# A four-layer graph network on one core: the planner that writes out the order of its instructions gets other costs, rules and ranks

## The chip, the core and the metric

The kernel runs on one core of a Trainium2 chip. The metric is the device time of one execution in microseconds (us), the median of several runs. TensorE (PE) multiplies, VectorE (DVE), ScalarE (ACT) and GpSimd (POOL) do the elementwise work, and the queue of SyncE (SP) issues nearly all transfers.

## What is computed

There are 128 batches. Each is a matrix x of 128 nodes by 512 features in float32; `adj` is one 128 x 128 matrix of edge weights for all of them. Four layers follow one another, each of the form `x = layernorm(x + layer(x))` over the features, with no dependence between batches:

```
layer 0:  A = adj @ x ; C = adj @ x + b ; out[:, n] = max over m of relu(A[:, m] + (C - A)[:, n])
layer 1:  q, k, v = x@Wq+bq, x@Wk+bk, x@Wv+bv ; 8 heads of 64
          softmax(q k^T / 8 + (1-adj) * -1e9) v, then @ Wo + bo
layer 2:  h = x@W ; e = leaky_relu(s1 + s2^T) * adj ; elu(softmax(e) @ h + beta*h)
layer 3:  (D^-1/2 adj D^-1/2) @ (x @ weight) + bias
```

With one adj for both weights of layer 0, its output is a row maximum of `adj @ x` plus b, cut off at zero.

## The kernel before, in words

**Batches in pairs.** Batches b and b+1 form a pair. The six products with 512 x 512 weights (Q, K, V, Y for Wo, U for layer 2's W, Z for layer 3's weight) are made once per pair with Strassen's scheme: `seven` (L619 ff.) writes seven half-size products P1 to P7 into three PSUM tiles px, py, pz. px holds P1 and then P2, py P6, P7, P4, and pz P5, P3. ScalarE copies P1 out (`u`, `uL`), VectorE makes U2, U3, C21, C22 and C12. GpSimd makes four sums S1 to S4 of the operand (L651). Three differences of weight quarters are made once per weight (`T`, L631 to L635): on VectorE for Q and K, on GpSimd for the others.

**Steps of one batch.** LD loads x (L411). A multiplies by adj (L764), R takes the row maximum (L770), ST0 the statistics (L581), Q0, P0 and AP0 normalise (L590 to L609; the power is on GpSimd, L604). MX1 writes x to a DRAM buffer dx (L788). RL reads it back as x2 for the residual (L802). For attention x must be turned to features by nodes: MX2 reads dx back in four transfers with 32-row blocks (L794) and TX turns the blocks on VectorE (L830). For the first pair only (`early`, b < 2) PX, PT and PTE do this without DRAM: a VectorE copy (L810), four TensorE transposes (L819), another copy (L824). SC makes the scores (L855), M, SM1, EXP, SMR, SMN the softmax (L871 to L900), MS1, MS2 and TS turn the probabilities through DRAM (L904, L912, L920), O multiplies them by v (L930). Then come Y, layer norm, the layer 2 attention (L, E, EZ, E1, EE, E2, BT, BE, GT), U, its elu (U1, UE, U2, UP), layer norm, NX (L1075), Z, layer norm and OUT (L1106). SC and O use half of TensorE's array (64 rows or columns), all other products use the whole.

**One-time steps.** Weights, biases and broadcast rows are fetched one after another on SP in the order of `FETCH`; Wq and its biases are fetched on ScalarE's queue ahead of everything else. ROW multiplies bv by Wo (L524). LOG makes ten VectorE instructions for layer 2's score vectors (L538, L543), LOG1 turns them on TensorE (L556). MASK, BQ and NORM prepare mask, scaled bias and normalised adj.

**The order.** Every engine works its queue strictly in order of issue, and the kernel writes that order itself. `STEPS` gives each step an engine, a cost in us, the steps it comes after, and the buffers it takes with the readers that free them (`POOLS` has their numbers; `+` is both batches of a pair, `-1` the batch before, `@` batches 0 and 1). `list_order` then plays the whole kernel: again and again it takes, of all steps whose inputs are listed, the one that can start first. On TensorE ties go to the lowest `rank`, which is the batch number plus the step's entry in `LAG`, less an entry in `LEAD` for the last pairs; on other engines to the step that was ready first, less its `soon`:

```
if s.engine == "PE":
    key = (t, rank(*k) - (CLOSE if mode and s.mode else 0.0), k)
else:
    key = (t, ready[k] - s.soon, k)
```

A transfer is an SP step of 0.4 us, whose reader is given a fixed delay (`("LD", 3.1)`). A switch between whole and half array costs 0.1. The planner decides only the order; on the chip, semaphores make each instruction wait for its inputs, and an instruction that waits holds up all behind it on its engine.

Of the kernel before, what the change touches and what calls it, by code (L numbers as in the profile page):

```python
# [10 lines left out]
ALU = mybir.AluOpType  # L11
# [3 lines left out]
S = 32  # L15
# [10 lines left out]
CLOSE = 0.5  # L26


class Step:
# [9 lines left out]
    def __init__(self, engine, cost, *after, takes=(), soon=0.0, batches=None, port=False, mode=""):  # L39
        self.port = port or engine == "POOL"  # L40
        self.mode = mode
        self.engine, self.cost, self.after = engine, cost, after
        self.takes, self.soon = dict(takes), soon
        self.batches = batches or (lambda b: True)
# [17 lines left out]
def list_order(steps, rank, pools, n):  # L62
# [5 lines left out]
    for s, b in todo:  # L68
        for a in steps[s].after:
            a, late = a if isinstance(a, tuple) else (a, 0.0)  # L70
            for k in steps[s].others(a, b):
                if k in todo:
                    missing[s, b].add(k)
                    users.setdefault(k, []).append(((s, b), late))
    can = {k for k in todo if not missing[k]}
    free, ends, taken, order, mode = {}, {}, {p: [] for p in pools}, [], ""
    while todo:
        best = None
        for k in can:
            s = steps[k[0]]  # L80
            t = max(ready[k], free.get(s.engine, 0.0), free.get("port", 0.0) if s.port else 0.0)
            for p in s.buffers(k[1]):
                if len(taken[p]) >= pools[p]:
                    for r in taken[p][-pools[p]]:
                        t = max(t, ends.get(r, 1e9) + SIGNAL)
            if t >= 1e9:
                continue
            if s.engine == "PE":
                key = (t, rank(*k) - (CLOSE if mode and s.mode else 0.0), k)
            else:  # L90
                key = (t, ready[k] - s.soon, k)
            if best is None or key < best:
                best = key
        t, _, k = best
        s = steps[k[0]]
        order.append((t, *k))
        ends[k] = t + s.cost
        if s.engine == "PE" and s.mode != mode:
            ends[k] += SWITCH
            mode = s.mode  # L100
        free[s.engine] = ends[k]
        if s.port:
            free["port"] = ends[k]
        todo.discard(k)
        can.discard(k)
        for p, readers in s.buffers(k[1]).items():
            ends_of = [r for a in readers for r in s.others(a, k[1])]
            taken[p].append([r for r in ends_of if r in missing])
        for u, late in users.get(k, ()):
            same = steps[u[0]].engine == s.engine and not late  # L110
            ready[u] = max(ready[u], ends[k] + late + (0.0 if same else SIGNAL))
            missing[u].discard(k)
            if not missing[u]:
                can.add(u)
# [11 lines left out]
def early(b):  # L126
    return b < 2


def late(b):  # L130
    return b >= 2
# [13 lines left out]
    "ROW": Step("PE", 3.5, "BV", ("BO", 4.0), takes={"tr": ("ROW1",)}, batches=first),  # L145
    "ROW1": Step("DVE", 0.7, "ROW", batches=first),
    "LOG": Step("DVE", 5.7, "BETA", ("A1", 4.0), batches=first, port=True),
# [7 lines left out]
    "LD": Step("SP", 0.4, "LD-1", ("LD-2", 8.0), takes={"x": ("MX1", "PX")}),  # L155
    "ST0": Step("DVE", 0.82, ("LD", 3.1), takes={"t0": ("AP0+",)}),
    "ADJ": Step("PE", 0.2, ("LD", 2.3), takes={"tr": ("ADJ1",)}, batches=first),
    "ADJ1": Step("DVE", 0.3, "ADJ", batches=first),
    "A": Step("PE", 0.87, ("LD", 3.1), "A-1", "ADJ1@", takes={"tr": ("R",)}),
    "R": Step("DVE", 0.82, "A", takes={"r": ("AP0+",)}),  # L160
    "Q0": Step("ACT", 1.2, "ST0+", "R+", soon=10, batches=even),
    "P0": Step("POOL", 0.58, "Q0", soon=10, batches=even),
    "AP0": Step("ACT", 1.03, "P0+", soon=20),
    "MX1": Step("SP", 0.4, "AP0", "MX1-1", takes={"dx": ("MX2+", "RL")}),

    "PX": Step("DVE", 0.6, "AP0", takes={"xB": ("PT",)}, soon=20, batches=early, port=True),
    "PT": Step("PE", 0.5, "PX", takes={"tr": ("PTE",)}, batches=early),
    "PTE": Step("DVE", 0.65, "PT", "PTE-1", soon=20, batches=early),
    "MX2": Step("SP", 2.6, ("MX1", 2.1), takes={"xB": ("TX",)}, batches=late),
    "RL": Step("SP", 0.4, ("MX1+", 2.1), takes={"x2": ("UP+",)}, batches=even),  # L170
    "C1": Step("POOL", 1.27, ("RL+", 3.0), "ROW1@"),
    "TX": Step("DVE", 0.65, ("MX2", 2.9), "TX-1", batches=late),
    "SC": Step("PE", 1.09, mode="row", takes={"sc": ("M",)}),
    "M": Step("DVE", 1.33, "SC", "MASK@", takes={"s": ("MS2",)}),
# [4 lines left out]
    "MS1": Step("SP", 0.4, "SMN", takes={"dp": ("MS2",)}),  # L179
    "MS2": Step("SP", 1.8, ("MS1", 2.7), takes={"sB": ("TS",)}),  # L180
    "TS": Step("DVE", 1.18, ("MS2", 3.8), takes={"sT": ("O",)}),
# [30 lines left out]
    "OUT": Step("SP", 0.4, "AP3"),  # L212
# [5 lines left out]
for i, name in enumerate(FETCH):  # L218
    STEPS[name] = Step("SP", 0.4, (FETCH[i - 1], 1.3) if i else ("LD@", 4.0), batches=first)
# [4 lines left out]
def sum_steps(n, engine_needs, readers):  # L224

    for i in range(4):
        needs = engine_needs if i == 0 else [f"{n}S{i}"]
        takes = {"SX" if n == "X" else "S": readers} if i == 0 else {}
        cost = 0.75
        STEPS[f"{n}S{i+1}"] = Step("POOL", cost, *needs, takes=takes, batches=even)  # L230


def seven_steps(n, sums, needs, weights, pool, out, add=(), turned=False, copy=False, T="POOL"):
# [10 lines left out]
    STEPS[n + "T"] = Step(T, 5.2 if T == "POOL" else 3.0, *weights, batches=first)  # L244
# [12 lines left out]
    step("P6", "PE", c, "S2", "P1", (n + "T@",), takes={"py": (n + "C21",)})  # L257
# [3 lines left out]
    step("P4", "PE", c, "U3")  # L261
# [25 lines left out]
for n, needs, letters in (  # L287
# [4 lines left out]
    "Q": seven_steps("Q", "X", ["TX+", "PTE+", "BQ@"], [("ADJ1", 9.0), "PTE+"], "xT", {"qT": ("SC+",)},  # L292
                     turned=True, T="DVE"),
    "K": seven_steps("K", "X", ["TX+", "PTE+", "BQ@"], [("WK3", 4.0)], "xT", {"kT": ("SC+",)},
                     turned=True, T="DVE"),
    "V": seven_steps("V", "X", ["TX+", "PTE+"], [("WV3", 4.0)], "xT", {"v": ("O+",)}, copy=True),
    "Y": seven_steps("Y", "Y", ["OE+"], ["ROW", ("WO3", 4.0)], "oT", {}, add=["C1+"]),
    "U": seven_steps("U", "U", ["GE+"], ["LOG", ("W23", 4.0)], "gT", {"x3": ("OUT+",)}, copy=True),
    "Z": seven_steps("Z", "Z", ["NE+"], [("W33", 4.0)], "nx", {}, add=["C3+"]),
}  # L300
STEPS["SC"].after = (*done["Q"], *done["K"])
# [7 lines left out]
    "A": 0.506, "QP4": 9.260, "KP1": 9.601, "QP1": 10.141, "QP6": 10.308, "QP2": 10.612,  # L309
    "QP7": 11.336, "QP5": 11.387, "QP3": 11.470, "KP6": 11.592, "KP2": 11.639,  # L310
    "KP7": 11.706, "KP4": 11.707, "KP3": 11.885, "KP5": 11.949, "VP6": 12.245, "SC": 12.416,
    "VP1": 13.139, "VP2": 13.218, "VP3": 13.390, "VP7": 13.434, "VP5": 13.540,
    "VP4": 13.603, "O": 15.187, "YP2": 16.207, "YP1": 16.635, "UP4": 16.678, "YP7": 16.681,
    "YP4": 16.877, "YP6": 17.006, "YP3": 17.007, "YP5": 17.021, "E": 17.459, "BT": 18.003,
    "GT": 18.470, "UP7": 18.991, "UP1": 19.286, "UP6": 19.912, "UP5": 20.037, "UP2": 20.403,
    "UP3": 20.409, "NX": 20.899, "ZP1": 22.103, "ZP6": 22.106, "ZP2": 22.151, "ZP3": 22.157,
    "ZP4": 22.409, "ZP7": 22.472, "ZP5": 22.856,
# [3 lines left out]
    "Q56": 0.53, "U56": 0.07, "A57": -0.03, "BT57": -0.1, "GT57": -0.06, "NX57": 2.33,  # L321
    "O57": -0.08, "Y57": 0.14, "BT58": -0.35, "E58": 0.31, "GT58": 0.72, "K58": 0.05,
    "NX58": -0.04, "O58": 0.4, "SC58": -1.4, "U58": 0.34, "V58": 1.06, "Y58": 2.36, "BT59": -0.24,
    "E59": -0.03, "K59": 0.5, "NX59": 1.93, "O59": 0.25, "Q59": -1.29, "SC59": 0.01, "U59": -0.55,
    "Y59": -0.04, "Z59": 0.01, "BT60": 0.03, "E60": 0.36, "GT60": 0.39, "K60": 0.03,
    "NX60": -0.22, "Q60": -0.03, "SC60": -0.01, "V60": 0.51, "A61": -3.65, "BT61": 0.32,
    "E61": 3.22, "GT61": -0.07, "K61": 2.69, "SC61": -0.11, "U61": -11.19, "V61": -0.03,
    "Y61": -0.11, "Z61": 0.22, "A62": -0.09, "BT62": -0.26, "E62": -0.69, "GT62": -1.7,
    "K62": 0.01, "NX62": 4.35, "O62": 0.18, "Q62": 0.09, "U62": -0.09, "V62": -3.72, "Y62": 0.36,
    "Z62": -0.17, "BT63": 5.89, "E63": 1.65, "K63": 0.46, "NX63": -0.37, "O63": 2.5, "Q63": -0.04,  # L330
    "SC63": 6.66, "U63": 0.09, "V63": -2.36, "Y63": -0.12, "Z63": -0.21,
# [11 lines left out]
def kernel(  # L343
# [117 lines left out]
    for part in (bq_part, bk_part, *wq_parts):  # L461
        fetch(nc.scalar, part)
# [156 lines left out]
    def seven(n, w, operand, sums, tag, result, added=None, bias=None, scale=1.0):  # L619
# [10 lines left out]
        def T(b):  # L630
            op = (nc.vector if n in "QK" else nc.gpsimd).tensor_tensor  # L631
            op(T3, W[1, 1], W[0, 1], ALU.subtract)
            op(T1, W[0, 1], W[0, 0], ALU.subtract)
            op(T2, W[1, 1], T1, ALU.subtract)
            op(T4, W[1, 0], T2, ALU.subtract)  # L635
# [114 lines left out]
        do[n + "T"], do[n + "u"], do[n + "uL"] = T, u, uL  # L750
# [368 lines left out]
    for i in range(2):  # L1119
        do[f"LOG1{'ab'[i]}"] = lambda b, i=i: LOG1(i)  # L1120
        do[f"LOG2{'ab'[i]}"] = lambda b, i=i: LOG2(i)
    with tc.manual_schedule():
# [46 lines left out]
```

## Time and profile before

| | |
|---|---|
| median of 3 runs | 3119.07 us (3118.03 to 3120.9) |
| the profiled execution | 3121.7 us, span of its instructions 3119.8 us |
| TensorE busy | 3059.5 us, 98% of the span, 21018 matmuls |
| VectorE, ScalarE, GpSimd busy | 2303.2 (74%), 2205.9 (71%), 1676.2 (54%) us |
| transfers | 312.91 MB, mean 100 GB/s |
| chain of work that ended last | PE 91%, DMA 3%, DVE 2%, ACT 2%, issue 1% |

"Busy" for TensorE is from the first to the last of pipelined matmuls, so a busy engine is not one at its peak. The granted clock (PEclk) is the share of full clock that TensorE got, 1.00 or 0.50 in any moment, and a mean in a stretch. In a line of the timeline the columns are start, duration, engine, source line, operation, what is written and read, shapes and the number of instructions merged. A bracket gives the idle time of the engine before it and what ended it. A line with SPq is SP's queue issuing a transfer. Names are those of the tiles: ps_a belongs to step A, px_Q to products P1 and P2 of Q, py_K to P6, P7, P4 of K, and so on; ps_x to PT, ps_wa to LOG1, ps_nx to NX. xB is MX2's target, x<-dx is RL.

### The profile page before, as it was taken

What the parts mean: (1) busy time and instruction counts of PE and PEld (TensorE: products, weight loads), DVE (VectorE), ACT (ScalarE), POOL (GpSimd) and SP (SyncE); (2) the same over time, 40 slices, a digit from 0 to 9 for tenths busy, and PEclk for the clock granted to TensorE, in tenths of its full rate; (3) what the DMA queues carried; (4) which work ended last, traced back from release to release, by engine and by line L of the source; (5) the groups of instructions that cost most, each with busy time, mean ns of one, the idle gap of its engine ahead of it and who ended that gap; (6) DMA issues with size and microseconds to landing.
All of it is one profiled execution on the core that took longest, in us unless ns stands there. A gap on an engine that the chain in (4) does not pass through costs nothing.

```text
span 3119.8 us, 61689 instructions
## 1 busy us (share of the span) xinstructions
PE 3059.5 (98%) x21018; PEld 2694.8 (86%) x21018; DVE 2303.2 (74%) x5416; ACT 2205.9 (71%) x7234; POOL 1676.2 (54%) x1946
## 2 busy tenths in 40 slices
PE   7999999999999999999999999999999999999996
PEld 4888888888888888888888888888888888898985
DVE  6777777777777777777777777777777777777774
ACT  3667777777777777777777777777777776776764
POOL 4344545555555555555555555555455555565565
PEclk8999999999999999999999999999999999999998
DMA  7432323323323323323333233233233232322220
GB/s 212 133 110 84 113 89 111 105 89 109 105 93 109 102 96 102 106 97 102 99 105 98 99 105 100 93 111 102 90 111 105 89 109 88 102 82 89 68 68 27
DMA packets 235611, 312.91 MB, mean 100 GB/s; under 512 B 27809, under 2 KB 157985, under 8 KB 235297
## 3 DMA queue, kind: packets, MB, share of 16 engines
q1 hardware_dynamic: 233520, 307.93, 30.3%
q8 instruction: 166, 2.72, 0.4%
q10 hardware_dynamic: 1776, 1.05, 0.2%
q14 instruction: 149, 1.21, 0.1%
HBM read 174.66 MB, written 134.22 MB: 99 GB/s over the span
## 4 chain that ended last, share of the span: by engine, by line
PE 91%; DMA 3%; DVE 2%; ACT 2%; issue 1%; POOL 0%; SPq 0%; POOLq 0%; DVEq 0%; ACTq 0%
PE py_Y L675 5%; PE py_U L675 5%; PE py_V L675 5%; PE py_Q L675 5%; PE py_Z L675 5%; PE py_K L675 5%; PE ps_s L855 4%; PE ps_o L930 4%; PE px_U L675 4%; PE ps_nx L1075 4%; PE pz_Q L675 4%; PE px_V L675 4%; PE px_Y L675 4%; PE ps_gT L1028 4%; PE pz_Y L675 3%; PE pz_Z L675 3%
## 5 line engine op out<-in xcount | busy, mean ns | idle before, releaser
L609 ACT ACTIVATE x<-x,off,rstd 128x512 f32<-128x512 f32 x512 | 416.7, 814 | 17.1
L886 ACT ACTIVATE s<-s,mx 128x128 f32<-128x128 f32 x1024 | 395.6, 391 | 27.3 <-DVE mx L880 27.3
L604 POOL TENSOR_TENSOR rstd<-rstd,neg_half 128x2 f32<-128x2 f32 x256 | 178.8, 699 | 388.9 <-ACT rstd L590 388.7
L581 DVE BATCH_NORM_STATS2 st<-x 128x6 f32<-128x512 f32 x512 | 349.1, 682 | 41.8 <-DMA x<-in_x 36.7
L900 ACT ACTIVATE s<-s,sm 128x128 f32<-128x128 f32 x1024 | 313.1, 391 | 19.7 <-DVE sm L895 19.6
L1089 POOL TENSOR_TENSOR x<-x,b_bc 128x512 f32<-128x512 f32 x128 | 163.2, 1276 | 255.4 <-PE ps_nx L1075 254.2
L1056 POOL TENSOR_TENSOR x<-x,x 128x512 f32<-128x512 f32 x128 | 163.6, 1278 | 176.6 <-DVE x L1052 169.9
L651 POOL TENSOR_TENSOR S_U<-gT 128x256 f32<-128x256 f32 x128 | 107.1, 836 | 228.0 <-ACT gT L940 228.0
L608 ACT ACTIVATE off<-off,rstd 128x1 f32<-128x1 f32 x512 | 145.5, 284 | 77.6 <-POOL rstd L604 77.5
L964 DVE SCALAR_TENSOR_TENSOR junk<-x,wa_bc 128x512 bf16<-128x512 f32 x256 | 184.2, 719 | 16.1 <-ACT x L609 10.6
L886 ACT ACTIVATION_READ_ACCUMULATOR s<-s,mx 128x1 f32 x1024 | 195.4, 191 | 0.0
L920 DVE STREAM_TRANSPOSE sT<-sB 128x1024 f32<-128x1024 f32 x128 | 159.2, 1244 | 34.9 <-PE ps_o L930 33.4
L651 POOL TENSOR_TENSOR S_Y<-oT 128x256 f32<-128x256 f32 x128 | 93.9, 733 | 139.8 <-PE pz_U L675 125.6
L806 POOL TENSOR_TENSOR x<-x,bo_bc 128x512 f32<-128x512 f32 x128 | 160.8, 1277 | 15.0 <-DMA x<-dx 14.8
L871 DVE TENSOR_TENSOR s<-ps_s,mask 128x512 f32<-128x512 f32 x256 | 163.4, 679 | 2.4 <-PE ps_s L855 2.1
L734 DVE TENSOR_TENSOR x<-py_U,u_U 128x256 f32<-128x256 f32 x192 | 81.1, 422 | 103.8 <-PE py_U L675 53.7
L880 DVE TENSOR_REDUCE mx<-s 128x8 f32<-128x1024 f32 x128 | 154.6, 1208 | 0.2
L675 PEld LDWEIGHTS px_Q<-xT,wq_sb 128*128 128x128 f32 x1024 | 129.3, 192 | 26.4 <-issue 23.7
L675 PEld LDWEIGHTS py_K<-SX_V,KT 128*128 128x128 f32 x1024 | 129.8, 193 | 24.5 <-issue 23.4
L855 PE MATMUL ps_s<-kT,qT 64*128 64x128 f32 x2048 | 148.9, 285 | 0.0
L1075 PE MATMUL ps_nx<-naT,x 128*128 128x128 f32 x1024 | 138.4, 280 | 10.5 <-ACT x L609 10.5
L855 PEld LDWEIGHTS ps_s<-kT,qT 64*128 64x128 f32 x2048 | 124.3, 187 | 26.1 <-issue 21.8
(186 smaller groups left out, 9116.0 us busy)
## 6 DMA issues: line engine op xcount, KB each, us to landing
dp<-s SPq DMA_DIRECT2D x128, 512.0 KB, 2.8
sB<-dp SPq DMA_DIRECT2D x512, 128.0 KB, 2.8
x<-in_x SPq DMA_DIRECT2D x128, 256.0 KB, 2.9
dx<-x SPq DMA_DIRECT2D x128, 256.0 KB, 2.1
x<-dx SPq DMA_DIRECT2D x64, 512.0 KB, 3.3
out_x<-x SPq DMA_DIRECT2D x128, 256.0 KB, 2.0
xB<-dx SPq DMA_DIRECT2D x504, 64.0 KB, 2.0
wk_sb<-in_L_gnn_Wk SPq DMA_DIRECT2D x4, 256.0 KB, 7.7
```

What stands on the lines that cost most here:

```text
L581: nc.vector.bn_stats(st, t)
L604: nc.gpsimd.tensor_tensor(r, r, neg_half.to_broadcast([P, 2]), ALU.pow)
L609: nc.scalar.activation(dst, src, AF.Identity, bias=shift, scale=scale)
L651: nc.gpsimd.tensor_tensor(s[:, i], x, y, op)
L675: nc.tensor.matmul(to, lhsT=one, rhs=two, start=(new and k == 0), stop=(k == 1), skip_group_check=True,)
L855: nc.tensor.matmul(scores[b][par][:, c, :], lhsT=qT[b][rows, c, cols], rhs=kT[b][rows, c, cols], start=True, stop=True,)
L871: nc.vector.tensor_tensor(by_head(s)[:, par * C : (par + 1) * C], ps.rearrange("p h (q s) -> p h q s", s=S), mask.rearrange("p (q s) -> p ...
L886: nc.scalar.activation(s[:, :, h], s[:, :, h], AF.Exp, bias=mx[:, h : h + 1], accum_out=sums[b][:, h : h + 1],)
L900: nc.scalar.activation(s[:, :, h], s[:, :, h], AF.Identity, scale=sm[:, h : h + 1])
L964: nc.vector.scalar_tensor_tensor(junk, x2[b][:, b % 2], 1.0, wa_bc[i], op0=ALU.mult, op1=ALU.mult, accum_out=s12[b][:, i : i + 1],)
L1056: nc.gpsimd.tensor_tensor(t, t, x2.pop(b)[:, b % 2], ALU.add)
L1075: nc.tensor.matmul(ps[:, c, :], lhsT=x3[b][:, b % 2, c * P : (c + 1) * P], rhs=naT, start=True, stop=True,)
```

## The change

The diff touches the planner, its tables, and the places that a step can be cut:

- **Costs of TensorE.** If TensorE was idle for more than REST = 1.4 us, steps that start within WAKE = 3.7 us cost double. A switch is counted only between whole and half array, not between SC and O. CLOSE, the bonus for a half-array step while the array is in halves, goes from 0.5 to 2.0 batches.
- **Transfers.** A step with `dma=(latency, time on the bus)` ends when a bus shared by all transfers has carried it. A reader without a delay of its own waits for that end.
- **rush.** On engines other than TensorE, steps of the first four batches' layer 0 and turning (40) and the operand sums of batches 0 and 2 (30) win ties. SP's MX1 has it too.
- **Turning.** `early` and `late` go from b < 2 to b < 4: batches 2 and 3 also take PX, PT, PTE instead of MX2, TX.
- **Weight sums.** T becomes four steps T0 to T3 of one instruction each (0.75 on VectorE, 1.34 on GpSimd). P6 needs T2, P4 needs T3.
- **Fetches.** The first eight pieces (Wk, Wv) follow each other by at least 1.0 us and start 2.0 us after the loads of batches 0 and 1 (1.3 and 4.0 before); the later ones follow by 3.0. Wq's four pieces become steps WQ0 to WQ3 on ScalarE.
- **Other.** SC also comes after the SC of the batch before; `s` is free after MS1, not MS2.
- **Ranks.** LAG and LEAD are new. A is 0.325 and the attention products lie 15.7 to 19.2 batches behind (9.3 to 13.6 before); the last Z product is at 28.3 (22.9). LEAD has 26 entries (62).

```diff
-CLOSE = 0.5
+CLOSE = 2.0
+REST, WAKE = 1.4, 3.7
...
-            a, late = a if isinstance(a, tuple) else (a, 0.0)
+            a, late = a if isinstance(a, tuple) else (a, None)
...
-                key = (t, ready[k] - s.soon, k)
+                key = (t, ready[k] - s.soon - (s.rush if k[1] < 4 else 0.0), k)
...
-        ends[k] = t + s.cost
-        if s.engine == "PE" and s.mode != mode:
-            ends[k] += SWITCH
+        cost = s.cost
+        if s.engine == "PE":
+            if t - free.get("PE", -9.0) > REST:
+                warm = t + WAKE
+            if t < warm:
+                cost *= 2
+            if bool(s.mode) != bool(mode):
+                cost += SWITCH
             mode = s.mode
-        free[s.engine] = ends[k]
+        ends[k] = free[s.engine] = issued = t + cost
+        if s.dma:
+            ends[k] = free["bus"] = max(t + s.dma[0], free.get("bus", 0.0)) + s.dma[1]
...
-            same = steps[u[0]].engine == s.engine and not late
-            ready[u] = max(ready[u], ends[k] + late + (0.0 if same else SIGNAL))
+            if steps[u[0]].engine == s.engine and not late and (late == 0.0 or not s.dma):
+                t = issued
+            elif late is None:
+                t = ends[k] + SIGNAL
+            else:
+                t = issued + late + SIGNAL
+            ready[u] = max(ready[u], t)
...
 def early(b):
-    return b < 2
+    return b < 4
...
-    "LD": Step("SP", 0.4, "LD-1", ("LD-2", 8.0), takes={"x": ("MX1", "PX")}),
-    "ST0": Step("DVE", 0.82, ("LD", 3.1), takes={"t0": ("AP0+",)}),
+    "LD": Step("SP", 0.4, ("LD-1", 0.0), ("LD-2", 8.0), takes={"x": ("MX1", "PX")}, dma=(2.55, 0.9)),
+    "ST0": Step("DVE", 0.82, "LD", takes={"t0": ("AP0+",)}, rush=40),
...
-    "A": Step("PE", 0.87, ("LD", 3.1), "A-1", "ADJ1@", takes={"tr": ("R",)}),
-    "R": Step("DVE", 0.82, "A", takes={"r": ("AP0+",)}),
+    "A": Step("PE", 0.87, "LD", "A-1", "ADJ1@", takes={"tr": ("R",)}),
+    "R": Step("DVE", 0.82, "A", takes={"r": ("AP0+",)}, rush=40),
...
-    STEPS[name] = Step("SP", 0.4, (FETCH[i - 1], 1.3) if i else ("LD@", 4.0), batches=first)
+    after = (FETCH[i - 1], 1.0 if i < 8 else 3.0) if i else ("LD@", 2.0)
+    STEPS[name] = Step("SP", 0.4, after, batches=first, dma=(2.5, 0.9 if name[0] == "W" else 0.1))
+for i in range(4):
+    after = ((f"WQ{i - 1}", 0.4),) if i else ()
+    STEPS[f"WQ{i}"] = Step("ACT", 0.1, *after, batches=first, dma=(2.5, 0.9))
...
-    STEPS[n + "T"] = Step(T, 5.2 if T == "POOL" else 3.0, *weights, batches=first)
+    for i in range(4):
+        after = [f"{n}T{i - 1}"] if i else weights
+        cost = 1.34 if T == "POOL" else 0.75
+        STEPS[f"{n}T{i}"] = Step(T, cost, *after, batches=first, port=True)
...
-STEPS["SC"].after = (*done["Q"], *done["K"])
+STEPS["SC"].after = ("SC-1", *done["Q"], *done["K"])
...
 LAG = {
-    "A": 0.506, "QP4": 9.260, "KP1": 9.601, "QP1": 10.141, "QP6": 10.308, "QP2": 10.612,
...
+    "A": 0.325, "QP2": 15.731, "QP7": 15.871, "QP1": 16.057, "QP6": 16.294, "KP6": 16.456,
+    "VP6": 16.608, "QP4": 16.618, "KP1": 17.099, "KP2": 17.121, "KP7": 17.182,
+    "KP4": 17.445, "QP5": 17.471, "QP3": 17.625, "KP5": 17.893, "SC": 17.957, "KP3": 18.214,
...
-    for part in (bq_part, bk_part, *wq_parts):
+    for part in (bq_part, bk_part):
         fetch(nc.scalar, part)
```

## The prediction

> **What bounds the kernel now.** I read the stretches first, then TensorE's waits, then the order of time around the longest of them. The stretches (time, busy time and instructions of TensorE, its weight loads, VectorE, ScalarE, GpSimd; granted TensorE clock, share of the DMA engines, GB/s):
>
> ```profile
> 0.00:30.00 30.00, 17.06 (x43) 9.37 (x44) 18.19 (x40) 6.79 (x19) 8.55 (x17) 0.74 0.93 233
> 30.00:60.00 30.00, 24.75 (x147) 19.03 (x146) 14.99 (x35) 11.47 (x35) 17.40 (x17) 0.96 0.63 184
> 60.00:80.00 20.00, 15.57 (x87) 11.99 (x86) 17.74 (x39) 10.64 (x41) 12.58 (x12) 0.85 0.71 220
> ...
> 300.00:2900.00 2600.00, 2598.80 (x18084) 2306.06 (x18083) 1946.31 (x4601) 1895.14 (x6223) 1420.73 (x1654) 1.00 0.31 100
> 2900.00:3050.00 150.00, 146.04 (x946) 126.83 (x945) 113.00 (x260) 98.82 (x310) 91.06 (x103) 0.99 0.20 66
> 3050.00:3119.80 69.80, 46.35 (x212) 38.30 (x210) 30.53 (x76) 31.37 (x74) 36.32 (x42) 0.86 0.07 27
> ```
>
> From 300 to 2900 us TensorE has no idle time at full clock; no other engine is above 75%. The timeline repeats there, every product of a pair 47.17 us after the same one of the pair before. 64 pairs x 47.17 = 3019, so about 100 us of the 3119.8 lie at the ends. To place them I gave each matmul record the mean distance to the next start that its kind has between 500 and 2500 us (sum 3023.0; the few one-time products at 0.1 each), and subtracted the sum so far from the clock. TensorE has lost 21.7 us at 30, 31.5 at 60, 39.7 at 80, 41.8 at 120, 55.2 at 300, 57.6 at 2900 and 96.8 at the end. So: start 55, middle 2.4, end 39. The lost time is idle time plus half pace, as the timeline of TensorE shows:
>
> ```profile
> 15.76 1.06 PE L819 MATMUL ps_x<-ident,xB 128*128 128x128 f32 x4
> ...
> 58.96 3.68 PE L764 MATMUL ps_a<-x,adjT 128*128 128x512 f32 x4 [4.11 <-DMA x<-in_x]
> ...
> 72.50 0.60 PE L556 MATMUL ps_wa<-ident,wa_col 128*128 128x128 f32 x4
> 76.08 2.05 PE L675 MATMUL py_Q<-SX_V,QT 128*128 128x128 f32 x8 [2.98 <-DVE qT L727]
> ...
> 270.48 1.97 PE L675 MATMUL pz_K<-SX_V,wk_sb 128*128 128x128 f32 x8 [2.77 <-DVE kT L727]
> ...
> 3098.13 3.78 PE L1075 MATMUL ps_nx<-naT,x 128*128 128x128 f32 x16 [5.67 <-ACT x L609]
> ```
>
> The bracket is the idle time and what ended it. After each long one a product takes double: eight py_Q 2.05 us against 1.06, sixteen ps_nx 3.78 against 2.1. The queue of the DMA issues shows why x was late at 58.96:
>
> ```profile
> 49.33 2.11 SPq L794 DMA_DIRECT2D xB<-dx  x4
> 51.48 0.43 SPq L802 DMA_DIRECT2D x<-dx  x1
> 51.95 0.43 SPq L411 DMA_DIRECT2D x<-in_x  x1
> ```
>
> The load of x is issued at 51.95 behind other transfers and lands 7.0 us later (chain of waits), where the page's median is 2.9; the engines are fully busy then (share 1.01 from 50 to 60 us).
>
> **The change, part by part.** It adds no arithmetic except transposes; it changes the order in which the queues are filled. The order follows from a planner, so I cost what the new rules can reach.
>
> *Middle.* The products are the same and the period holds no idle time. The change there can only be in switching between full products and the half-array ones (SC, O). In the timeline a visit "O then SC" costs about 0.09 to enter, 0.15 between, 0.2 after: 0.44. There are 149 visits in the trace, where 128 (two per pair) are needed if each O has its SC beside it. The larger CLOSE can pair the 21 SC and 21 O that stand alone: a lone visit costs 0.29, two 0.58, so 21 x 0.14 = 3 us at most, most of it before 300 us. SC and O cannot be chained longer: one score buffer waits for M (two evictions of 0.68) and one sT for the transpose of 1.24 us. Middle: 0.
>
> *Start, to 30 us (21.7 lost).* With rush, layer 0 of batches 0 to 3 goes ahead on VectorE, GpSimd and SP. The chain of waits shows GpSimd's pow for the degrees (0.57) ahead of rstd: about 0.85 us. Batch 1's xT waits behind the statistics of batch 3, whose x is late: 0.8. Wk goes out as one run instead of being split by x and dx, whose issue waits: its last part is issued at 13.04 and px_K starts at 20.21, 1.9 after xT is complete at 18.3; the first K product comes 3 us earlier with both. SP then stands from 14.06 to 19.19 on the reload of dx, whose landing takes 5.4 us because the bus is full; the loads of batches 4 and 5 and the rest of Wv stand behind it. The planner now knows that the landing is late and issues loads first: the wait before A at 25.72 (1.47) and the half pace after it (A 2.04 for 1.02) go. The weight sums in four steps let xT copies and evictions slip between: VectorE's four of QT take 0.69 to 1.10 each, so a queue of 4.1 us becomes one of 1.1. The sums themselves are no shorter. Wq's four issues move from the prologue into the list, but stay on ScalarE's queue, where nothing else is due before the first rstd at 7.90 (they end at 7.79): 0; were rstd put ahead of them, K's and Q's sums would wait some 2 us more. SP gets no issue it did not have. Added up 0.85 + 0.8 + 1.9 + 2.5 = 6 us.
>
> *30 to 60 (9.8 lost).* 2.7 of it is ROW (3.5 us for eight products, counted at 0.8), which stays. The wait of 4.11 and the half pace after it (1.8) are what the change aims at. Turning pair 1 on TensorE takes away 8 issues of 0.43 = 3.4 us on SP ahead of that load and 0.5 MB (1.9 us at 275 GB/s); weights after Wv go out every 3 us instead of as fast as SP can. I take 4.5 of the 5.9. What it adds: 8 transposes. Four take 0.44 at full pace (72.50, the next product starts at 72.94) and 1.06 at half. The Trainium skill, "TensorE: Matmul & The Clock Gate", Part 4, speaks against this: transposes do not count as TensorE work for the clock, so they would neither run at full clock nor keep it. By that 8 cost 2.1 us plus up to 1.7 for products after them; by the row of 72.50, 0.9. The row decides: a stream of products had just run there, as it will here. VectorE pays 0.43 + 0.69 for PX and PTE where TX was 0.70: 0.8 us for both batches, beside TensorE. Net -3.5 (between +1 and -5).
>
> *60 to 80 (8.2 lost).* Most comes from LOG: its ten VectorE instructions run from 67.0 to 75.6, 8.6 us where the planner counts 5.7 before and after, and the eviction of qT stands behind them (wait 2.98, half pace 1.7). LOG is not split. Fewer DMAs in the way: -1 (0 to -3).
>
> *80 to 300 (15.5 lost).* Waits of 0.3 to 2.8 us, mostly a VectorE queue whose head waits for x (st at 269.21 waits for x, kT behind it, TensorE 2.77, then 1.7 for half pace). A planner with a bus sees such landings. I take 5 of the 15.5 and 1 for SC beside O: -6 (0 to -10).
>
> *End (39 lost).* After the last pair's U products come U1, exp, U2, UP, statistics, rstd: TensorE waits 5.67 (and 4.78 for the pair before) and restarts at half pace (ps_nx 3.78 twice: 3.4 us; others at 3046 and 3102 about 3). After its Z products 9 us of eviction, statistics and output remain whatever the order. Only Z products of the pair before can fill the gap, about six of 0.866. The planner now sees half pace, so it gains by keeping some back. I take 4.5, between +5 (new ranks fit the end worse) and -12.
>
> The rule against the planner's own assumption: it sets half pace after 1.4 us of idle time. The same page (Part 1) says after a window of about 3.4 us without work. Rows: 1.45, 1.52 and 1.73 us of waiting (at 70.67, 127.44, 156.05) were followed by products of 1.13 us, single pace; waits of 2.77 and more were followed by half pace each time, and so was one of 1.57 at 3044.86, after two shorter ones. So 1.4 is somewhat too wary; a planner that spends order on harmless gaps of 1.5 us loses perhaps 1 us, already in the ranges.
>
> **Sum.** -6 -3.5 -1 -6 +0 -4.5 = -21 us. The profiled execution was 3121.7 (span 3119.8), 2.6 over the median 3119.07; the difference is applied to the median: 3098.
>
> **The rivals.** (a) *The expected order, likeliest:* 3098, own range 3086 to 3109. (b) *The wait moves:* the load of x is no longer late, but LOG, ROW and the softmax of the first pairs are; the first 60 us gain half (5), the rest and the end 4: 3110. For it: LOG unchanged at 8.6 us against 5.7 planned. Against it: only 5 of the 55 us hang on LOG. (c) *More than that:* TensorE has work from about 16 us on and loses 25 at the start (12 to the first K product, 3 restarting, ROW 3, some 7 in fill), 2 in the middle and 30 at the end: 57 in place of 97, -40 or 3079. For it: the granted clock and the waits leave that much. Against it: every misjudged landing would have to go, and LOG stays. (d) *Slower: the new ranks leave no room in the repeating part.* In LAG the second product of Q (15.731) now ranks ahead of the first (16.057), where it stood 0.47 batches, 11 us, behind (10.141 and 10.612); K's two are 0.02 apart (2.04 before); SC (17.957) ranks before K's P3 (18.214), which it needs. They start the moment the planner believes their input is there. A wait that is met late costs 0.10 us even when short (px_Y takes 0.97 to the next product in each period where the others take 0.865). The price is 0.1 per product and pair, 64 pairs: 6.4 us each. From 0.33 us a pair, between three and four such places, it eats the 21; with four, 25.6 us, the time is 3119 - 21 + 26 = 3124. Against it: ranks with no room exist before as well (Q's P4 at 9.260 before its P7 at 11.336, U's P4, Z's P2), and only px_Y and pz_Q show it.
>
> **How the numbers follow.** (a) 0.63, (b) 0.19, (c) 0.10, (d) 0.08. A change of 0.2% (6.2 us) is about what a measurement of this kernel can tell from none. Faster by more: (a), (c) and most of (b), 0.84; within: 0.08; slower: 0.08. The range reaches from just short of (c)'s middle, 3080, to past (b), 3114.
>
> **What would show it.** Right: lost time at 30 us near 16, at 80 near 29, at 300 near 39; no wait of A for x over 2 us; px_K before 18 us; a period of 47.17 between 500 and 2500. Wrong: a period above 47.3 (d); the same 40 lost at 80 us with LOG or ROW ahead of the wait (b); an end that loses over 42 us. If the start gains under 8 us, the bus was not what held it.

## The result and the profile after

The changed kernel takes 3107.11 us (median of 6 runs, 3106.0 to 3109.07), the kernel before 3120.07 beside it. The ratio is 0.9958, 95% interval 0.9945 to 0.9971: 13 us faster, between 9 and 17. The forecast was 3098 with a range from 3080 to 3114. The profiled execution has a span of 3106.0 us where the one before had 3119.8.

The stretches of the changed kernel, columns as before:

```profile
0.00:30.00 30.00, 14.30 (x30) 6.75 (x30) 15.65 (x41) 8.42 (x23) 7.09 (x18) 0.72 0.85 213
30.00:60.00 30.00, 29.36 (x192) 23.60 (x192) 23.69 (x49) 13.11 (x43) 15.40 (x15) 1.00 0.68 210
60.00:80.00 20.00, 19.84 (x167) 17.91 (x165) 14.94 (x36) 18.24 (x71) 11.72 (x13) 1.00 0.69 218
...
300.00:2900.00 2600.00, 2599.62 (x18076) 2322.69 (x18075) 1982.97 (x4585) 1897.24 (x6196) 1444.58 (x1653) 1.00 0.30 99
2900.00:3050.00 150.00, 141.19 (x891) 120.60 (x891) 110.83 (x259) 93.28 (x288) 93.37 (x104) 0.99 0.17 57
3050.00:3106.00 56.00, 36.62 (x151) 29.15 (x149) 19.91 (x45) 21.77 (x50) 26.79 (x29) 0.80 0.08 28
```

From 30 to 80 us TensorE runs 359 matmuls at full clock; before it ran 234 with gaps. The first 30 us are worse, 30 matmuls for 43. The repeating part looks the same and holds 8 matmuls less in 2600 us (18076 for 18084). The timeline shows where the first 30 us go, and that nothing long is left after them:

```profile
16.54 2.07 PE L784 MATMUL ps_a<-x,adjT 128*128 128x512 f32 x2 [5.40 <-DMA x<-in_x]
20.20 1.12 PE L839 MATMUL ps_x<-ident,xB 128*128 128x128 f32 x4 [1.58 <-DVE xB L830]
...
25.44 1.91 PE L693 MATMUL px_Q<-xT,wq_sb 128*128 128x128 f32 x8
...
30.64 1.16 PE L693 MATMUL px_Q<-xT,wq_sb 128*128 128x128 f32 x8 [1.09 <-ACT uL_Q L706]
31.64 0.60 PE L839 MATMUL ps_x<-ident,xB 128*128 128x128 f32 x4
32.07 1.06 PE L693 MATMUL py_Q<-SX_V,QT 128*128 128x128 f32 x8
```

The same account of lost time as in the prediction, with the kernel before's mean distance for each kind of matmul, gives the table. "End" is what is lost after 2900 us; the period is the mean distance from a pair's products to the next pair's between 500 and 2500 us (for the kernel before the usual one; a single longer step lifts its mean to 47.19). "Planned" is the same loss at 300 us in the list that the kernel's own planner makes: 300 less the costs of TensorE's steps that it starts before. The times come from several chips, so the ratio to the kernel before, run beside each, is what compares. The weights of the kernel before give the changed kernel 33.7 at 300 us; its own give 32.7, which some of the expectations below name.

| kernel | us | ratio (95%) | lost at 30 | at 300 | planned | 300 to 2900 | end | period |
|---|---|---|---|---|---|---|---|---|
| before | 3120.1 | 1 | 21.7 | 55.2 | 28.4 | 2.4 | 39.2 | 47.17 |
| changed | 3107.1 | 0.9958 (0.9945-0.9971) | 22.9 | 33.7 | 25.9 | 5.3 | 43.1 | 47.25 |
| one pair turned on TensorE | 3116.4 | 0.9976 (0.9967-0.9985) | 22.9 | 42.1 | 34.0 | 5.0 | 44.1 | 47.26 |
| no shared bus | 3125.8 | 1.0007 (0.9999-1.0015) | 26.0 | 51.3 | 34.7 | 5.3 | 43.1 | 47.27 |
| before + new ranks | 3278.5 | 1.0492 (1.0473-1.051) | 18.4 | 53.4 | 31.3 | 135.9 | 64.6 | 49.90 |
| no rush | 3119.5 | 0.9988 (0.9981-0.9994) | 22.8 | 43.3 | 40.3 | 4.8 | 44.1 | 47.26 |
| no half pace | 3117.9 | 0.9982 (0.9975-0.9989) | 22.2 | 44.9 | 33.0 | 4.4 | 42.1 | 47.25 |
| sums in one step | 3124.2 | 1.0007 (0.9999-1.0015) | 26.0 | 49.4 | 38.6 | 4.5 | 43.7 | 47.25 |
| fetches as before | 3118.2 | 0.9989 (0.9983-0.9996) | 20.5 | 45.4 | 39.4 | 4.8 | 43.3 | 47.25 |
| LEAD empty | 3116.4 | 0.9978 (0.997-0.9987) | 22.9 | 34.1 | 25.9 | 5.3 | 51.2 | 47.26 |
| K's P7, Z's P5 moved | 3130.6 | 1.0022 (1.0015-1.003) | 22.9 | 33.9 | 25.9 | 26.6 | 43.3 | 47.70 |
| Z's P5 moved | 3104.9 | 0.9943 (0.993-0.9955) | 22.9 | 35.7 | 25.9 | 0.8 | 44.1 | 47.16 |
| Z's P5, E moved | 3100.3 | 0.9928 (0.9915-0.9942) | 22.9 | 34.8 | 25.9 | -3.4 | 43.2 | 47.07 |
| the same, new LEAD | 3093.2 | 0.9906 (0.9892-0.9919) | 22.9 | 35.2 | 25.9 | -3.7 | 35.5 | 47.07 |

Six kernels keep the changed kernel's start list and show 33.7 to 35.7 at 300 us: differences under 2 us there mean nothing. So the start gained 21.5 us, and the middle gave back 2.9 and the end 3.9. Of these 21.5 only 2.5 are in the plan (28.4 to 25.9). For the other 19 the chip now keeps closer to its plan: it loses 7.8 us more than planned, where it lost 26.8 more before.

### The profile page after: what moved, and what is told of

Read it like the earlier page. It is cut to its first block, busy times and chain, and to the rows that moved or that the text cites. A ratio compares the mean times of both kernels' runs of the same rounds, so it can differ in the third digit from the quotient of the medians.

```text
span 3106.0 us, 61445 instructions
## 1 busy us (share of the span) xinstructions
PE 3058.3 (98%) x21026; PEld 2709.3 (87%) x21026; DVE 2346.7 (76%) x5418; ACT 2216.0 (71%) x7234; POOL 1700.1 (55%) x1946
## 4 chain that ended last, share of the span: by engine, by line
PE 95%; DVE 1%; DMA 1%; POOL 1%; ACT 1%; issue 1%; ACTq 0%; POOLq 0%; SPq 0%; DVEq 0%
PE py_Q L693 6%; PE py_V L693 6%; PE py_K L693 5%; PE py_U L693 5%; PE py_Y L693 5%; PE py_Z L693 5%; PE ps_s L875 4%; PE ps_o L950 4%; PE px_Y L693 4%; PE px_K L693 4%; PE ps_nx L1095 4%; PE pz_K L693 4%; PE px_Q L693 4%; PE px_U L693 4%; PE ps_gT L1048 4%; PE pz_Q L693 4%
## 5 line engine op out<-in xcount | busy, mean ns | idle before, releaser
L984 DVE SCALAR_TENSOR_TENSOR junk<-x,wa_bc 128x512 bf16<-128x512 f32 x256 | 230.0, 898 | 16.4 <-ACT x L625 5.5
L669 POOL TENSOR_TENSOR S_U<-gT 128x256 f32<-128x256 f32 x128 | 117.2, 915 | 189.9 <-ACT gT L960 189.7
L606 ACT ACTIVATE rstd<-mv,eps_c 128x2 f32<-128x2 f32 x256 | 75.6, 295 | 200.6 <-DVE mv L598 194.0
L940 DVE STREAM_TRANSPOSE sT<-sB 128x1024 f32<-128x1024 f32 x128 | 158.8, 1240 | 35.7 <-PE ps_o L950 35.5
L624 ACT ACTIVATE off<-off,rstd 128x1 f32<-128x1 f32 x512 | 147.2, 288 | 21.5 <-POOL rstd L620 21.4
L1040 ACT COPY bT<-ps_bT 128x128 f32<-128x128 f32 x128 | 33.9, 265 | 175.9 <-PE ps_bT L1035 175.6
L1095 PEld LDWEIGHTS ps_nx<-naT,x 128*128 128x128 f32 x1024 | 131.6, 195 | 29.3 <-issue 23.0
L752 DVE TENSOR_TENSOR x<-py_Z,x 128x256 f32<-128x256 f32 x192 | 80.4, 419 | 90.0 <-PE py_Z L693 87.1
```

The costliest lines, as they stand in the source:

```text
L669: nc.gpsimd.tensor_tensor(s[:, i], x, y, op)
L984: nc.vector.scalar_tensor_tensor(junk, x2[b][:, b % 2], 1.0, wa_bc[i], op0=ALU.mult, op1=ALU.mult, accum_out=s12[b][:, i : i + 1],)
L1095: nc.tensor.matmul(ps[:, c, :], lhsT=x3[b][:, b % 2, c * P : (c + 1) * P], rhs=naT, start=True, stop=True,)
```

## The experiments

**The start: one part taken back at a time.** In each the planner makes a new list with the changed ranks, so what is seen is the part and the new list together.

```diff
 def early(b):
-    return b < 4
+    return b < 2
```

> The changed kernel with batches 2 and 3 turned through DRAM again (early is b < 2), planned anew. Theory A (the start is quicker because loads and turned inputs come in time, the turning being part of it): TensorE has lost 36 to 37 us at 300 us in place of 32.7, time about 3111. Rival B (a planner that knows of the bus orders the transfers well enough without it): lost 32 to 34 at 300, time within 1.5 us of 3107.

Lost at 300 us 42.1, ratio 0.9976. Up to 80 us it loses no more than the changed kernel (26.3 for 27.2); 15.8 of its 42.1 us come between 80 and 300, where the changed kernel loses 6.5. Rival B falls. Theory A has the sign, but neither the size nor the place: the turning was to free SP before 60 us, and its lack shows only later.

```diff
-            ends[k] = free["bus"] = max(t + s.dma[0], free.get("bus", 0.0)) + s.dma[1]
+            ends[k] = t + s.dma[0] + s.dma[1]
```

> The changed kernel, whose planner gives each transfer its latency and its time alone, with no sharing of the bus. Theory A (the shared bus is what puts the loads in the right place): at least half of the 22.5 us goes, lost at 300 us 43 or more, time 3117. Rival B (rush, the order of the fetches and the new ranks do it): lost at 300 us at most 36, time 3107 to 3110.

Lost 51.3: 17.6 of the 21.5 us are gone, as A has it. 7.2 of them are lost by 60 us (33.5 for 26.3), and the other 10.4 later, nearly all between 80 and 120. For the first part the page of waits (TensorE, 0 to 60 us) and VectorE's timeline name the wait:

```profile
PE ps_naT L529 <- DVE e_na_rows L524: 15.2, 1, 15.2
```
```profile
7.03 0.18 DVE L598 BATCH_NORM_AGGREGATE mv<-st 128x2 f32<-128x6 f32 x1
18.20 0.69 DVE L652 TENSOR_TENSOR QT<-wq_sb 128x512 f32<-128x512 f32 x1 [10.98 <-DMA x<-in_x]
```

Without a bus the planner believes that Wq is there at 5.7 us and lists Q's first difference of weights ahead of R, NORM and all the rest; VectorE stands at it for 11 us (the bracket names x; what it needs is Wq), and TensorE behind NORM. With the bus the planner puts it at 9.8, behind R and NORM. That is still too early: it runs at 17.65, and what is listed behind it waits in the changed kernel too (more on this below). The 7.2 us were not planned: up to 60 us both lists lose 17.6. The 10.4 after 60 us are another matter, since this kernel's planner itself expects to lose 8.8 more there.

The kernel before with only LAG and LEAD of the changed one:

> The kernel before with only LAG and LEAD of the changed one. Theory A (the planner's costs and rules make the start): lost at 300 us 50 or more, as before (55.2), time 3115 or more. Rival B (the ranks alone, with Q ahead of K and A further ahead): lost at 300 us 33 to 40, time 3100 to 3110.

Lost 53.4 at 300 us: the ranks alone make no better start. They also ruin the middle (49.90 us a pair). TensorE's waits:

```profile
PE ps_a L757 <- DMA x<-in_x: 69.2, 36, 4.4
PE ps_a L757 <- ACT s L879: 35.2, 19, 2.8
```

A is first in rank; the old planner lists it a fixed 3.1 us after its load, and on the chip it waits 36 times at the head of TensorE's queue. The new ranks are worth nothing with the old costs. The reverse, the new planner with the old ranks, was not run on the chip; that planner's own list would end at 3178 us, where it ends at 3092 with the new ranks. So neither half stands alone.

```diff
-                key = (t, ready[k] - s.soon - (s.rush if k[1] < 4 else 0.0), k)
+                key = (t, ready[k] - s.soon, k)
```

> The changed kernel without rush (ties on the other engines go to the step that was ready first, in all batches), planned anew. Theory A (rush brings layer 0 and the turning of the first pairs forward, which the later start lives on): lost at 300 us 37 to 41 by the weights of before, where the changed kernel has 33.7, time 4 to 7 us above it. Rival B (the order follows from the landings, rush decides few ties): lost within 1.5 us of 33.7.

Lost 43.3, more than A gave, but not where A has it: up to 80 us it equals the changed kernel (26.7 for 27.2). Between 80 and 120 it loses 11.7 us where the changed kernel loses 3.4, with one wait of A for x of 3.7 us. Up to there TensorE gets no more work for rush.

```diff
-REST, WAKE = 1.4, 3.7
+REST, WAKE = 1e9, 3.7
```

> The changed kernel, whose planner never counts half pace, planned anew. Theory A (half pace matters where TensorE waits often, at the end): the last 200 us lose 3 to 6 us more than the changed kernel's 43, the start stays within 2. Rival B (the planner's threshold of 1.4 us is off and the end gains nothing by it): the end loses 43 or less, the time is within 2 us of the changed kernel.

Both fall. Without half pace in the planner the end loses 42.1, 1 us less, which means little (kernels with the same LEAD lie between 43.1 and 44.1); the start is 11.2 us worse, all of it after 60 us (25.2 there, for 26.3).

The four differences of a weight in one step:

> The changed kernel with each weight's four differences as one step again (3.0 us on VectorE, 5.36 on GpSimd), planned anew. Theory A (copies and evictions that slip between the four matter in the first 100 us): lost at 300 us 36 to 42 by the weights of before, where the changed kernel has 33.7 and the one with Y moved 35.7; time 4 to 7 us above the changed kernel. Rival B (VectorE has nothing else due then): 33 to 36.

Lost 49.4, 15.7 us more, beyond A. For 7.0 of them the place is the one meant: 26.0 at 30 us, 33.3 at 60 in place of 26.3. Most of the others come after 120 us. VectorE's timeline, with GpSimd's differences beside it:

```profile
24.53 1.75 DVE L649 TENSOR_TENSOR KT<-wk_sb 128x512 f32<-128x512 f32 x1
26.31 1.63 DVE L649 TENSOR_TENSOR wk_sb<-wk_sb 128x512 f32<-128x512 f32 x1
27.98 1.63 DVE L649 TENSOR_TENSOR KT<-wk_sb 128x512 f32<-128x512 f32 x1
29.65 0.69 DVE L649 TENSOR_TENSOR KT<-wk_sb,KT 128x512 f32<-128x512 f32 x1
30.26 0.68 DVE L840 COPY xT<-ps_x 128x512 f32<-128x512 f32 x1
```
```profile
22.84 1.49 POOL L649 TENSOR_TENSOR VT<-wv_sb 128x512 f32<-128x512 f32 x1 [11.49 <-DMA wv_sb<-in_L_gnn_Wv]
...
27.48 1.59 POOL L649 TENSOR_TENSOR VT<-wv_sb,VT 128x512 f32<-128x512 f32 x1
```

The copy that frees the transposes' buffer stands behind all four, of which the three that run beside GpSimd's take about 1.7 us each, and TensorE waits 6.0 us for it.

```diff
-    after = (FETCH[i - 1], 1.0 if i < 8 else 3.0) if i else ("LD@", 2.0)
+    after = (FETCH[i - 1], 1.3) if i else ("LD@", 4.0)
```

> The changed kernel with the fetches spaced as before (1.3 us each, from 4.0 us after the first loads), planned anew. Theory A (the run of Wk ahead of the loads of batches 2 and 3 is what kept the first 30 us from gaining; the wide spacing of the later weights is what helps after them): lost at 30 us 19 to 21 in place of 22.9, at 300 us 37 or more in place of 33.7. Rival B (with a bus in the planner the spacing hardly matters): within 1.5 us of 22.9 and of 33.7.

A holds at both ends: 20.5 at 30 us in place of 22.9, so the early run of Wk costs 2.4 us of the first 30; and 45.4 at 300, lost between 60 and 120. Start and spacing of Wk and the spacing of the later weights changed together here.

Together the six single parts lose 8.4 + 17.6 + 9.6 + 11.2 + 15.7 + 11.7 = 74 us where the start gained 21.5. They don't add. For the bus and the four steps about 7 us each sit by 60 us at a wait that the part was to prevent. All the rest appears later, from 60 or 80 us on, in a list made anew with ranks not fitted to it. The column "planned" tells how much of it the planner expects itself: without the turning, rush, the four steps or the spacing it plans 8 to 14 us more lost at 300 than in the changed list, and the chip keeps as close to these plans as to the changed one (3 to 11 us over, for 7.8). So what is lost there is mostly a poorer list. The bus and half pace are different: without them the chip loses 16.6 and 11.9 us more than planned. They make the plan truer. What rush, turning, steps and spacing are worth isn't settled; it would take ranks fitted again for each, which wasn't tried. CLOSE can be ruled out without a run: with 0.5 the changed planner makes the same list, and there are 149 visits to the half array, as before.

**The middle.** P1 of U and P1 of Y cost more than others. Groups of TensorE's instructions from 500 to 2500 us (busy us, mean ns, idle before) in the changed kernel:

```profile
L693 PE MATMUL px_Y<-wo_sb,oT 128*128 128x256 f32 x336 | 90.1, 391 | 0.0
L693 PE MATMUL px_U<-w_sb,gT 128*128 128x256 f32 x336 | 90.1, 390 | 0.0
...
L693 PE MATMUL px_V<-wv_sb,xT 128*128 128x256 f32 x336 | 86.2, 379 | 0.0
```

One matmul in eight takes 471 ns for 379, the first of P1. (In the kernel before both took 483, but U's P1 stood right behind a visit to the half array, whose price other products pay now; Y's P1 did not.) In the trace U's P1 begins its weight load at 1012.93; ScalarE's copy of K's P2 out of px, the one buffer they share, ends at 1012.88. In the planner's list both P1 start with 0.07 us to spare. Two products moved ahead of them in the finished list:

```diff
+        for step, filler in ((("UP1", b), ("KP7", b + 8)), (("YP1", b), ("ZP5", b - 6))):
+            if 0 < place[filler] - place[step] < 60:
+                moves[step] = filler
```

> The changed kernel; in the list that the planner returns, K's P7 is moved ahead of U's P1 and Z's P5 ahead of Y's P1 in the pairs of the repeating part, so that each P1 starts a product (0.87 us) later than its input is due. Nothing else moves. Theory A (P1 of U and of Y meet an input that is just late, at about 0.1 us each, and P6 of U 0.04): the period goes from 47.25 to 47.03, 49 pairs x 0.22 = 11 us, time 3096. Rival B (the 0.08 us that the period has gained belongs to the new alternation of SC, O and O, SC): the period stays within 0.03 of 47.25, time 3107.

Both waits go, and the period rises to 47.70: the middle loses 21 us more (26.6 for 5.3). TensorE's waits from 500 to 2500 us:

```profile
PE ps_bT L1051 <- DVE e L1044: 6.7, 21, 0.3
PE pz_K L709 <- DVE qT L761: 0.9, 6, 0.2
```

K's P7 stood eight products later; moving it shifts all eight by 0.89 us. My reading is that U's evictions shift with them at the head of VectorE's queue, so that the layer 2 softmax behind them is late for its turning; the waits shown are 7.6 of the 19 us that these 42 pairs lose, so the reading is not shown for the rest. Neither theory foresaw it. So the shift was made as small as could be: for Y only P5 of Z, its neighbour.

> The changed kernel with only Z's P5 moved ahead of Y's P1 in 49 pairs, two neighbours in the list, so that nothing else is shifted. Theory A (a product's late input costs 0.09 us, and a shift of 0.87 for two products alone moves no other wait): period 47.25 to 47.16, 4.5 us less than the changed kernel. Rival B (any shift uncovers a wait elsewhere, as the larger move did): period 47.25 or above.

Period 47.158, middle 0.8 in place of 5.3: 4.5 us, as A has it. (The times say the same, ratio 0.9943 for 0.9958, but their intervals overlap.) Then for U, instead of a product, E with its one transpose of 0.11 us:

```diff
-        for step, filler in ((("UP1", b), ("KP7", b + 8)), (("YP1", b), ("ZP5", b - 6))):
+        for step, filler in ((("UP1", b), ("E", b + 2)), (("YP1", b), ("ZP5", b - 6))):
```

> The kernel with Z's P5 ahead of Y's P1, and besides E (0.11 us) ahead of U's P1 in 49 pairs. In the trace U's P1 waits for px, which ScalarE's copy of K's P2 frees 0.05 us before. Theory A (0.11 us of cover is enough, and a shift of 0.11 for seven products uncovers nothing): period 47.158 to 47.03 to 47.07, 4 to 6 us less than with Y's P1 alone. Rival B (as with the move of K's P7, waits appear elsewhere): period 47.15 or above.

Period 47.07, the middle 4.2 us less again. The same two groups in this kernel:

```profile
L709 PE MATMUL px_Y<-wo_sb,oT 128*128 128x256 f32 x340 | 87.2, 379 | 0.0
L709 PE MATMUL px_U<-w_sb,gT 128*128 128x256 f32 x336 | 86.3, 379 | 0.0
```

**The end.** LEAD emptied:

> The changed kernel with LEAD empty, so that the last pairs keep the ranks of all others. Theory A (LEAD orders the end to some profit, if less than before): the last 200 us lose 47 to 50 in place of 43, time 4 to 7 us above the changed kernel. Rival B (the end's entries fit a planner that is wrong there): 43 or less.

The end loses 51.2 in place of 43.1: the entries (25 of them; the kernel before has 69) are worth 8 us, more than A had. Then new entries, searched with the changed planner, on top of both moves:

> The kernel with both moves and a new LEAD for the last pairs, searched with the changed planner, which plans the end 4.9 us earlier with it. Theory A (the planner's end is near enough to the chip's that order searched in it transfers): the last 200 us lose 38 to 41 in place of 43.1, time 2 to 5 us below the kernel with both moves. Rival B (the end's small waits differ from the plan): 43 or more.

The end loses 35.5, and 3093.2 us is the fastest kernel of the study, ratio 0.9906: 28.5 us under the kernel before on its chip. The planner had foreseen 4.9 us for the new entries; the chip gives 7, more than A had.

## Why the prediction was right, and where it was not

The sign, the sum's range and the place of the gain were right: the start. Its sizes were not, and two terms had the wrong sign, one of them (to 30 us) among the largest. That the sum lies in the range is in part luck: the start gave 5 us more than forecast, the middle and the end together 11.3 us less. Of the signs named in advance only the lost time at 80 (27.2 for 29) came. The 16 at 30 us, no wait of A over 2 us, a first product before 18 us and a period of 47.17 did not, and the loss at 300 was smaller than named (33.7 for 39). One sign of being wrong came too: an end that loses over 42 us (43.1).

| step | forecast | measured |
|---|---|---|
| to 30 us | -6 | +1.2 |
| 30 to 60 | -3.5 | -6.4 |
| 60 to 80 | -1 | -7.3 |
| 80 to 300 | -6 | -9.0 |
| middle | 0 | +2.9 |
| end | -4.5 | +3.9 |

(The eight transposes count as 0.8 us of work in this account, so the sum is 0.9 off the difference of the spans.)

*To 30 us.* "The first K product comes 3 us earlier" failed: the first product (now Q's) starts at 25.44, 5.2 later than K's before. VectorE's queue shows why. The same copy for the turning of batch 0, before and after:

```profile
12.66 0.43 DVE L810 COPY xB<-x 128x512 f32<-128x512 f32 x1 [0.44 <-ACT x L609]
```
```profile
17.65 0.69 DVE L652 TENSOR_TENSOR QT<-wq_sb 128x512 f32<-128x512 f32 x1 [6.89 <-DMA x<-in_x]
...
19.72 0.42 DVE L830 COPY xB<-x 128x512 f32<-128x512 f32 x1
```

Its x is ready at 12.1, but three differences of weights are listed ahead of it, and VectorE stands 6.9 us at the first, which needs Wq. Wq's last part lands at 17.46 (again the bracket names x; in the run with the fetches as before it names wq_sb at the same instruction). The forecast had the weight sums in four steps let such copies slip between; it left out that the planner, even with its bus, lists the first of them for 9.8 us, long before Wq lands. Besides, the run of Wk goes out at once, and the loads of batches 2 and 3 stand behind it and Wq: issued from 6.23 us on, their A starts at 16.54 after 5.40 us of waiting. With the fetches at their old spacing that A starts at 12.66 and the first difference at 16.47, and 2.4 us less are lost.

*30 to 80 us.* The step was right and too small, beyond both of its ranges. I took 4.5 of the 5.9 us for the late x; all of it went. LOG was the error: "LOG is not split", so its wait and half pace were to stay. It still holds VectorE's queue for 6.9 us (77.8 to 84.7), but the new list has TensorE's products of other pairs ahead of the eviction, and it costs one wait of 0.43. A block on a queue costs what is due behind it, not its length. The clock adds: after 28.2 us it is at full pace until 3038.8, where before it fell to half three more times (at 59.0, 76.1 and 270.6).

*Transposes.* The row decided rightly. Four take 0.43 us to the next start (31.64 to 32.07) at granted clock 1.00, in a stream of products.

*The middle.* Rival (d)'s mechanism is real, its places were not: Q's and K's second products and SC show no wait. U's P1 does, by 0.09 us a pair, about a quarter of what would have made the kernel slower, and one product on py_U by 0.04. Y's P1 had its wait before already.

*The end.* I expected the planner's knowledge of half pace to pay here. The run without it shows that it doesn't with these entries in LEAD (42.1 for 43.1). What the new list has that the old one had not is seen in TensorE's waits:

```profile
PE py_Z L693 <- POOL S_Z L669: 5.0, 2, 2.6
PE ps_nx L1095 <- ACT x L625: 3.8, 2, 2.7
...
PE py_U L693 <- POOL S_U L669: 2.6, 1, 2.6
```

The long waits of NX (10.5 us before) have shrunk to 3.8, but P6 of Z and U now waits 7.6 us for GpSimd's sums, which it waited 1.2 for before. The bound of +5 held. That it is a matter of the entries in LEAD and not of the ranks as such, the last experiment shows.

Rival (b)'s time, 3110, is nearer to the result than mine, and its 5 us for the first 60 are what they gained (5.2). But its mechanism is not what happened: the next 240 us gained another 16, where it had 4 for all the rest, and no long wait moved to LOG or ROW.

## What to carry to other kernels

When a list of instructions is planned, compare the plan's losses with the chip's stretch by stretch: most of the gain here came from a truer plan, not from a better one. Model what is shared (the bus): a transfer believed to have landed puts a stalled instruction at the head of a queue, and all behind it waits. Then look whether such an instruction is left; here Wq's still is. Where one engine is full and the list repeats, look for instructions that are met by their buffer within a tenth of a us: their price is multiplied by the repeats, and a tiny independent step put in front is a safer cover than a large one, whose shift uncovers other waits. Ranks, costs and rules are one thing; taking one back without fitting the others tells whether a wait returns, not what the part is worth. The plan of the new list tells which of the two one sees.

## What the runs showed of the hardware

- A buffer freed just in time costs its user 0.09 us even where no engine is seen idle: the first matmul of U's P1 takes 471 ns for 379, its weight load starting 0.05 us after the buffer is free. Cover of 0.11 us removes all of it.
- With the DMA engines full (share 1.07 from 6 to 17 us) a load of 256 KB takes long: issued at 6.23, batch 2's x landed at 16.50, where the median is 3.2 us. SP's next issue waited 2.4 us for a landing of Wq, which ScalarE's queue had issued.
- VectorE's differences of weights take 0.69 us alone and 1.63 to 1.75 with GpSimd's own differences beside them (four in one step).
- At the end waits of 1.07, 1.25 and 1.06 us left the clock at 1.00, one of 2.46 brought half pace (py_Z 2.07 for 1.03).
